# A four-direction scan network on one core: statistics loads on another queue, coefficients in pinned stages, larger scaling pieces, a prologue that loads first

## The chip, the cores and the metric

The kernel runs on one core of a Trainium2 chip. The core has TensorE (PE, matrix products), VectorE (DVE), ScalarE (ACT) and GpSimd (POOL). SyncE (SP) issues DMA copies; ACT issues some too, from its own queue, in the order of its own instructions. The metric is the device time of one execution in microseconds (us). The profile is of one execution, with the time of every instruction and copy.

## The reference

The input is x[32, 48, 64, 128] (batch, channel, row, column), float32. Two layers follow each other, each x = x + scan(gn(x)). gn is a group norm: 16 groups of 3 channels, mean and variance over channels, rows and columns of one batch entry. The scan has four sweeps; a step of a sweep adds to its input a 1-d convolution (5 taps, 48 to 48 channels) of the step before, along the other axis:

```python
def step(w, b):
    def f(carry, inp):
        nxt = inp + _conv1d(carry, w, b)
        return (nxt, nxt)
    return f
...
_, d_rest = jax.lax.scan(step(down_w, down_b), d0, xs[1:])      # down the rows
...
_, u_rest = jax.lax.scan(step(down_w, down_b), u0, seq)         # up the rows
...
_, r_rest = jax.lax.scan(step(right_w, right_b), r0, ws[1:])    # right over the columns
...
_, l_rest = jax.lax.scan(step(left_w, left_b), l0, R[Ww - 2::-1])  # left
...
x = x + _L0_conv_ref(_gn(x), ...)
x = x + _L1_conv_ref(_gn(x), ...)
```

Every step needs the one before it, so a sweep is a chain of 63 steps (rows) or 127 steps (columns).

## The kernel before

The 32 batch entries are 4 groups of 8. A pass is one layer of one group; there are 8 passes, layer 0 first. In a pass come 63 down steps, 63 up steps, 127 right and 127 left steps (`scans`, L505). A row step (`row_step`, L443) is 9 matmuls of 128x128 by 128x128 and 3 DVE operations that add the input row (L462). A column step works in two halves of 4 batch entries, each 3 matmuls (L476 to L480) and one DVE operation (L483).

One large SBUF tile, `arena`, holds the data of a pass. For rows it is read as `rows`, 64 rows of 384 numbers on 128 partitions. For columns it is read as `cols`, which begins 20 rows further (SHIFT) and has another layout on 112 partitions. So after the up sweep `hand_over` (L364) copies rows into `cols` by DMA, arena to arena, 20 copies (two parities of the row, ten pieces) for 8 rows; the last ones are split (`SPLITS`) at rows 4, 2 and 0. The parity r = 1 goes out on ACT's queue if the chunk ends at row 8 or below, all else on SP.

Around the scans stand helpers, Python generators that are advanced at given steps. `prepare` (L298) loads x of the next layer-0 group, reorders it with POOL copies (L331) from tiles `nat` to `perm` and stores it to DRAM as `xin`. `input_moments` and `result_moments` (L270, L285) load the data again into `perm` and let ACT sum values and squared deviations (`collect`, L190), with two small POOL operations (L199, L200) between. `scaling` (L212) turns these into a scale and an offset: small DVE operations, matmuls with a group mask (L223, L241) and a square root on ACT (L255). `fetch` (L347) loads a chunk of rows into the arena from `xin` (layer 0) or `mid` (layer 1) and scales it in place with 24 ACT operations (L356), one for each of 3 row blocks and 8 batch entries. `drain` (L491) adds the residual of the pass before in 16 steps during the next pass's row sweeps: it loads a piece into `nat`, adds on POOL (L382, L388) and stores to `mid` or to the output. Each drain step gives free 2048 numbers of `cols`, 5.3 rows, and the late fetches (rows 20 to 63) follow it. Rows 0 to 19 are outside `cols` and are fetched earlier, in the column sweeps. The last pass has `last_residual` (L402) in place of a drain.

Program order isn't the order of execution. A planner (the Tile framework's scheduler) simulates the program when it is built and fixes the order of each engine and queue: of the instructions that its simulation has ready it takes the one that comes first in the program. So an operation can stand far ahead of its place; in the profile the statistics loads of group 2, written in pass 1, start at 713.7 us, in pass 0's column sweeps. On the chip each engine and each queue then keeps that order and waits where something is late.

Of the kernel before, what the change touches and what calls it, by code (L numbers as in the profile page):

```python
# [30 lines left out]
F32 = mybir.dt.float32  # L31
# [11 lines left out]
GB = 8  # L43
# [9 lines left out]
LOADS = tuple(slice(a, b) for a, b in ((0, 4), (4, 12), (12, 20))) + tuple(  # L53
    slice(a, min(a + 8, 64)) for a in range(20, 64, 8)
)
EARLY = 3
SPLITS = {4: 8, 2: 4, 0: 2}
# [28 lines left out]
def kernel(  # L86
# [93 lines left out]
    class Moments:  # L180


        def __init__(self, parts: int, n: int, key: str):
            self.T, self.n, self.key = parts, n, key
            mean = stat_tile(GB * parts, f"mean{parts}", key)
            dev2 = stat_tile(GB * parts, f"dev2{parts}", key)
            self.mean = mean.rearrange("p (b t) -> p b t", t=parts)
            self.dev2 = dev2.rearrange("p (b t) -> p b t", t=parts)

    def collect(mo, t: int, views, key: str):  # L190


        bs = slice(min(views), max(views) + 1)
        for b, view in views.items():
            nc.scalar.activation(  # L195
                view, view, AF.Identity, scale=sides, accum_out=mo.mean[:, b, t : t + 1]
            )
        neg = stat_tile(GB, "neg", key)
        nc.gpsimd.tensor_scalar(neg[:, bs], mo.mean[:, bs, t], -1.0 / mo.n, None, ALU.mult)  # L199
        nc.gpsimd.tensor_scalar(  # L200
            mo.mean[:, bs, t], mo.mean[:, bs, t], 1.0 / mo.n, None, ALU.mult
        )
        for b, view in views.items():
            nc.scalar.activation(  # L204
                view,
                view,
                AF.Square,
                bias=neg[:, b : b + 1],
                accum_out=mo.dev2[:, b, t : t + 1],
            )  # L210

    def scaling(mo):  # L212

        key, T = mo.key, mo.T
        ps = ps_stat.tile([FULL, NG + 1, 2 * GB], F32, tag="ps_stat", name=f"ps_{key}")
        pair = stat_tile(2 * GB, "pair", key)
        if T > 1:
            total = stat_tile(GB, "total", key)
            nc.vector.tensor_reduce(total, mo.mean, mybir.AxisListType.X, ALU.add)
            nc.vector.tensor_scalar(pair[:, 0:GB], total, 1.0 / T, None, ALU.mult)  # L220
        else:
            nc.vector.tensor_copy(pair[:, 0:GB], mo.mean[:, :, 0])  # L222
        nc.tensor.matmul(ps[0:P, NG, 0:GB], mask_sb, pair[:, 0:GB], start=True, stop=True)  # L223
        mean_p = stat_tile(GB, "mean_p", key)
        nc.vector.tensor_copy(mean_p, ps[0:P, NG, 0:GB])
        dev = stat_tile(GB * T, f"dev{T}", key).rearrange("p (b t) -> p b t", t=T)
        nc.vector.tensor_tensor(
            dev, mo.mean, mean_p.unsqueeze(2).to_broadcast([P, GB, T]), ALU.subtract
        )
        sq = stat_tile(GB * T, f"sq{T}", key).rearrange("p (b t) -> p b t", t=T)  # L230
        nc.vector.tensor_tensor(sq, dev, dev, ALU.mult)
        all_sq = stat_tile(GB * T, f"all{T}", key).rearrange("p (b t) -> p b t", t=T)
        nc.vector.scalar_tensor_tensor(all_sq, mo.dev2, 1.0 / mo.n, sq, ALU.mult, ALU.add)
        if T > 1:
            total2 = stat_tile(GB, "total2", key)
            nc.vector.tensor_reduce(total2, all_sq, mybir.AxisListType.X, ALU.add)
            nc.vector.tensor_scalar(pair[:, GB:], total2, 1.0 / T, None, ALU.mult)
        else:
            nc.vector.tensor_copy(pair[:, GB:], all_sq[:, :, 0])
        for o in range(NG):  # L240
            nc.tensor.matmul(ps[:, o], maskp[:, o], pair, start=True, stop=True)  # L241
# [7 lines left out]
        var = small("var")  # L249
        nc.vector.tensor_scalar(var, ps[:, 0:NG, GB:], GN_EPS, None, ALU.add)  # L250
        mean = small("mean")
        nc.vector.tensor_copy(mean, ps[:, 0:NG, 0:GB])

        std = small("std")
        nc.scalar.activation(std, var, AF.Sqrt)  # L255
        r0 = small("r0")
        nc.vector.reciprocal(r0, std)
        t0 = small("t0")
        nc.vector.tensor_tensor(t0, var, r0, ALU.mult)
        t1 = small("t1")  # L260
        nc.vector.tensor_tensor(t1, t0, r0, ALU.mult)
        t2 = small("t2")
        nc.vector.tensor_scalar(t2, t1, -0.5, 1.5, ALU.mult, ALU.add)
        scale = small("scale", 2 * NGRP)
        nc.vector.tensor_tensor(scale, r0, t2, ALU.mult)
        offset = small("offset", 2 * NGRP)
        nc.vector.scalar_tensor_tensor(offset, mean, -1.0, scale, ALU.mult, ALU.mult)
        return scale, offset

    def input_moments(g: int):  # L270

        parts, n = 2, H * W // 4
        mo = Moments(parts, n, f"x{g}")
        coeffs[0, g] = mo
        for b in range(GB):
            for t in range(parts):
                tile_ = perms[t].rearrange("p r n -> p (r n)")
                flat = x[g * GB + b].rearrange("c (s t h) w -> s t c (h w)", s=2, t=parts)
                for s in range(2):
                    nc.sync.dma_start(tile_[SIDES[s]], flat[s, t])  # L280
                collect(mo, t, {b: tile_}, f"x{g}_{b}{t}")
                yield
        coeffs[0, g] = scaling(mo)

    def result_moments(g: int):  # L285

        mo = Moments(NCH, W * CH, f"m{g}")
        src = stages[1][g].rearrange("(q r) c n -> r c q n", r=2)
        for j in range(NCH):
            t = perms[j % 2]  # L290
            for r in range(2):
                nc.sync.dma_start(t[SIDES[r]], src[r, :, CH * j : CH * (j + 1)])
            view = t.rearrange("p q (n b) -> p b (q n)", b=GB)
            collect(mo, j, {b: view[:, b] for b in range(GB)}, f"m{g}_{j}")
            yield
        coeffs[1, g] = scaling(mo)

    def prepare(g: int):  # L298

        first = g == 0
        if first:
            at = H * ROW + 7 * CH * PAIR
            st = arena[0:P, at : at + GB * NCH * 6].rearrange(
                "p (b j k) -> p b j k", b=GB, j=NCH
            )
        for j in range(NCH):
            nat, perm = nats[j % 2], perms[j % 2]
            if first and j >= 2:  # L310
                at = H * ROW + CH * PAIR * (j - 2 if j < 9 else j - 16)
                nat = arena[0:P, at : at + CH * PAIR].rearrange("p (r n) -> p r n", r=CH)
                eng = nc.vector if j % 2 else nc.gpsimd
                eng.memset(nat[32:64], 0.0)
            h0 = 2 * CH * j
            nat = nat.rearrange("p r n -> p (r n)").rearrange("p (b n) -> p b n", b=GB)
            for s in range(2):
                h = h0 + s * CH
                nc.sync.dma_start(
                    nat[SIDES[s]],  # L320
                    x[g * GB : (g + 1) * GB, :, h : h + CH].rearrange(
                        "b c h w -> c b (h w)"
                    ),
                )
            if first:
                for b in range(GB):
                    nc.vector.bn_stats(st[:, b, j, :], nat[:, b])
            nat = nat.rearrange("p b (r k e) -> p r e k b", r=CH, e=E8)
            perm5 = perm.rearrange("p r (e k b) -> p r e k b", e=E8, k=NK)
            for r in range(CH):  # L330
                nc.gpsimd.tensor_copy(perm5[:, r], nat[:, r])  # L331
            for s in range(2):
                h = h0 + s * CH
                nc.sync.dma_start(
                    stages[0][g][h : h + CH].rearrange("h c n -> c h n"), perm[SIDES[s]]
                )
            yield
        if first:
            mo = Moments(1, 1, "x0")
            mv = stat_tile(2 * GB, "mv", "x0").rearrange("p (b k) -> p b k", k=2)  # L340
            for b in range(GB):
                nc.vector.bn_aggr(mv[:, b], st[:, b].rearrange("p j k -> p (j k)"))
            nc.vector.tensor_copy(mo.mean[:, :, 0], mv[:, :, 0])
            nc.vector.tensor_copy(mo.dev2[:, :, 0], mv[:, :, 1])
            coeffs[0, 0] = scaling(mo)

    def fetch(layer: int, g: int, j: int, scale, offset):  # L347

        hs = LOADS[j]
        src = stages[layer][g][hs].rearrange("h c (e n) -> e c h n", e=E8)  # L350
        for e, c0, c1, o, p0 in PIECES:
            nc.scalar.dma_start(rows[p0 : p0 + c1 - c0, hs, o], src[e][c0:c1])
        view = rows[:, hs].rearrange("p h o (k b) -> p o b h k", b=GB)
# [10 lines left out]
    def hand_over(h0: int, h1: int):  # L364

        qs = slice(h0 // 2, h1 // 2)
        for r in range(2):
            eng = nc.scalar if r and h1 <= RB else nc.sync
            src = rows[:, h0:h1].rearrange("p (q r) o n -> r o p q n", r=2)
            dst = cols[SIDES[r], qs].rearrange("p q e k b -> e p q (k b)")  # L370
            for e, c0, c1, o, p0 in PIECES:
# [161 lines left out]
    for _ in prepare(0):  # L533
        pass
# [111 lines left out]
```

## Time and profile before

| what | value |
|---|---|
| median of 3 runs | 5951.42 us (5949.96 to 5955.78) |
| the profiled execution | 5961.04 us, span 5959.3 us |
| busy: PE, DVE, ACT, POOL | 4860.6, 2548.1, 1812.3, 1087.5 us |
| mean granted TensorE clock | 0.922 |
| DMA | 599.97 MB, mean 101 GB/s |
| first row step | 229.7 us |
| last column step ends | 5810.4 us |

The stages are read from PE's instructions by tile: `row_01d` is layer 0, group 1, down; `col_12r` is layer 1, group 2, right. Sweeps in us:

| pass | down | up | gap | right | left |
|---|---|---|---|---|---|
| 00 | 138.5 | 126.8 | 55.9 | 173.5 | 170.4 |
| 01 | 146.3 | 126.8 | 45.1 | 172.1 | 170.4 |
| 02 | 146.3 | 126.8 | 44.9 | 173.1 | 170.4 |
| 03 | 155.3 | 127.7 | 47.2 | 172.7 | 240.6 |
| 10 | 148.6 | 126.8 | 46.4 | 226.4 | 170.4 |
| 11 | 170.5 | 126.8 | 50.9 | 172.0 | 232.5 |
| 12 | 169.2 | 126.8 | 52.8 | 172.7 | 170.4 |
| 13 | 171.7 | 126.8 | 48.3 | 172.7 | 170.4 |

A busy share is an average over stages with different limits; what a change in one stage is worth is read from that stage. Waits are put down to what ended last.

### The profile page before, as it was taken

How to read it: one execution, taken by the hardware profiler on the slowest of the kernel's cores; microseconds unless marked ns; L12 is line 12 of the kernel's file. 1: busy time of each engine (PE TensorE's matmuls, PEld its weight loads, DVE VectorE, ACT ScalarE, POOL GpSimd, SP SyncE). 2: the span in 40 equal slices, each digit the busy share in tenths (PEclk: the TensorE clock that was granted, in tenths of full speed). 3: DMA queues.
4: the chain of work that ended last, by engine and by line, in shares of the span. 5: the costliest groups of instructions: out<-in, count | busy, mean ns of one | idle time of the engine just before them, and what ended most of it. 6: DMA issues, size and time to landing. Idle time of an engine off the chain costs nothing. (4 is left out here: it accounts for less than half of the span.)

```text
span 5959.3 us, 105466 instructions
## 1 busy us (share of the span) xinstructions
PE 4860.6 (82%) x42592; PEld 4846.2 (81%) x42592; DVE 2548.1 (43%) x7387; ACT 1812.3 (30%) x3977; POOL 1087.5 (18%) x640
## 2 busy tenths in 40 slices
PE   0496999889996998795997969869698799986990
PEld 0496999889996998795997969869698799986990
DVE  3343554445443553342543535335354345433550
ACT  0451234024220396077050840308603020220000
POOL 3101303121221303000030001510015100350043
PEclk9998999999998999897998989989799899998995
DMA  7665838477465738442184412754117510463045
GB/s 149 118 114 108 174 64 184 106 155 151 98 158 109 167 66 192 111 84 54 22 184 109 84 19 44 149 122 83 30 34 151 121 37 1 95 129 89 1 69 92
DMA packets 847369, 599.97 MB, mean 101 GB/s; under 512 B 267584, under 2 KB 783680, under 8 KB 842272
## 3 DMA queue, kind: packets, MB, share of 16 engines
q1 hardware_dynamic: 603840, 483.73, 39.7%
q10 hardware_dynamic: 243040, 109.49, 9.5%
q8 instruction: 335, 5.49, 0.4%
q14 instruction: 154, 1.26, 0.1%
HBM read 341.31 MB, written 150.99 MB: 83 GB/s over the span
## 5 line engine op out<-in xcount | busy, mean ns | idle before, releaser
L356 ACT ACTIVATE arena<-arena,offset_m,scale_m 128x128 f32<-128x128 f32 (+1 forms) x864 | 425.6, 584 | 1243.6 <-DMA arena<-mid 895.1
L356 ACT ACTIVATE arena<-arena,offset_x,scale_x 128x128 f32<-128x128 f32 (+1 forms) x864 | 422.4, 590 | 901.2 <-DMA arena<-xin 738.6
L195 ACT ACTIVATE perm<-perm,sides 112x256 f32<-112x256 f32 (+1 forms) x560 | 476.2, 858 | 577.1 <-DMA perm<-in_x 192.4
L388 POOL TENSOR_TENSOR perm<-arena,nat 112x1024 f32<-112x1024 f32 x96 | 360.8, 3785 | 1154.8 <-DVE arena L483 459.7
L382 POOL TENSOR_TENSOR nat<-arena,nat 112x2048 f32<-112x2048 f32 x64 | 289.2, 4533 | 671.5 <-DMA nat<-xin 353.9
L204 ACT ACTIVATE perm<-perm,neg_m 112x256 f32<-112x256 f32 x512 | 381.0, 752 | 13.7 <-POOL neg_m L199 13.7
L331 POOL COPY perm<-nat 112x1024 f32<-112x1024 f32 x100 | 200.0, 2034 | 646.7 <-DMA nat<-in_x 599.8
L199 POOL TENSOR_SCALAR neg_m<-mean_m 112x8 f32<-112x8 f32 x64 | 15.1, 236 | 1250.1 <-ACT perm L195 1250.1
L424 POOL TENSOR_TENSOR perm<-arena,nat 112x256 f32<-112x256 f32 x108 | 114.4, 1067 | 485.4 <-DVE arena L483 328.1
L223 PE MATMUL ps_x<-pair_x,mask_sb 112*112 112x8 f32 x8 | 1.6, 276 | 237.2 <-DVE pair_x L222 221.4
L223 PEld LDWEIGHTS ps_x<-pair_x,mask_sb 112*112 112x112 f32 x8 | 1.5, 231 | 237.4 <-DVE pair_x L222 221.4
L476 PE MATMUL col_10r<-arena,wc 112*112 112x128 f32 x508 | 106.3, 292 | 97.3 <-DVE arena L483 50.9
L454 PE MATMUL row_13d<-arena,wd 128*128 128x128 f32 x1134 | 141.7, 291 | 30.0 <-DVE arena L462 30.0
L454 PEld LDWEIGHTS row_13d<-arena,wd 128*128 128x128 f32 x1134 | 139.1, 206 | 32.5 <-DVE arena L462 32.5
L454 PE MATMUL row_11d<-arena,wd 128*128 128x128 f32 x1134 | 137.7, 286 | 29.9 <-DVE arena L462 29.9
L454 PEld LDWEIGHTS row_11d<-arena,wd 128*128 128x128 f32 x1134 | 135.2, 201 | 32.0 <-DVE arena L462 32.0
L454 PE MATMUL row_12d<-arena,wd 128*128 128x128 f32 x1134 | 138.6, 287 | 27.7 <-DVE arena L462 27.7
L454 PEld LDWEIGHTS row_12d<-arena,wd 128*128 128x128 f32 x1134 | 136.0, 202 | 29.8 <-DVE arena L462 29.8
L476 PE MATMUL col_03l<-arena,wc 112*112 112x128 f32 x508 | 105.5, 290 | 67.2 <-DVE arena L483 67.2
L476 PE MATMUL col_11l<-arena,wc 112*112 112x128 f32 x508 | 105.4, 290 | 59.2 <-DVE arena L483 59.2
L454 PE MATMUL row_03d<-arena,wd 128*128 128x128 f32 x1134 | 137.1, 286 | 18.2 <-DVE arena L462 18.2
L454 PEld LDWEIGHTS row_03d<-arena,wd 128*128 128x128 f32 x1134 | 135.2, 201 | 20.0 <-DVE arena L462 19.8
(228 smaller groups left out, 13956.7 us busy)
## 6 DMA issues: line engine op xcount, KB each, us to landing
arena<-arena SPq DMA_DIRECT2D x672, 96.0 KB, 2.5
xin<-perm SPq DMA_DIRECT2D x128, 384.0 KB, 5.2
nat<-xin SPq DMA_DIRECT2D x128, 384.0 KB, 8.6
mid<-nat SPq DMA_DIRECT2D x128, 384.0 KB, 5.1
perm<-mid SPq DMA_DIRECT2D x128, 384.0 KB, 6.3
nat<-in_x SPq DMA_DIRECT2D x100, 384.0 KB, 8.0
perm<-in_x SPq DMA_DIRECT2D x96, 384.0 KB, 6.3
nat<-mid SPq DMA_DIRECT2D x96, 384.0 KB, 6.9
```

The costliest lines, as they stand in the source:

```text
L195: nc.scalar.activation(view, view, AF.Identity, scale=sides, accum_out=mo.mean[:, b, t : t + 1])
L199: nc.gpsimd.tensor_scalar(neg[:, bs], mo.mean[:, bs, t], -1.0 / mo.n, None, ALU.mult)
L204: nc.scalar.activation(view, view, AF.Square, bias=neg[:, b : b + 1], accum_out=mo.dev2[:, b, t : t + 1],)
L223: nc.tensor.matmul(ps[0:P, NG, 0:GB], mask_sb, pair[:, 0:GB], start=True, stop=True)
L331: nc.gpsimd.tensor_copy(perm5[:, r], nat[:, r])
L356: nc.scalar.activation(view[:, o, b], view[:, o, b], AF.Identity, bias=offset[:, o, b : b + 1], scale=scale[:, o, b : b + 1],)
L382: nc.gpsimd.tensor_tensor(nat, res, nat, ALU.add)
L388: nc.gpsimd.tensor_tensor(perm[:, t].rearrange("p (b k e) -> p b k e", b=GB, k=NK), cols[:, q + t].rearrange("p e k b -> p b k e"), nat[:, ...
L424: eng.tensor_tensor(perm[:, t].rearrange("p (b k e) -> p b k e", b=GB, k=kn), cols[:, q + t, :, ks].rearrange("p e k b -> p b k e"), nat[: ...
L454: nc.tensor.matmul(ps[o][:, a:b], wd[:, n], prev[:, i, a + s * GB : b + s * GB], start=seen[o] == 1, stop=seen[o] == left[o],)
L476: nc.tensor.matmul(ps, wt[:, 1], prev, start=True, stop=False)
```

## The change

- Statistics loads (`input_moments`, `result_moments`) are issued from ACT's queue, `fetch`'s loads from SP's. `collect` negates the mean with one ACT operation in place of two on POOL.
- `scaling` becomes a generator of eight stages. Its PE and DVE instructions are put behind the latest step's last matmul and DVE operation in the planner's order (`tc.issue_after`, which sets order and no wait). It is advanced in the right sweep from i = 60 (passes 0 to 3) or in the row sweeps from t = 30 (from pass 4 on).
- The pieces that `fetch` scales become (0, 4), (4, 12), (12, 20), (20, 28), (28, 44), (44, 64). Its loads are still of 8 rows at most. A late piece is fetched, as before, after the drain step that frees its last row; the first three are advanced at i = 100, 80, 60 of the left sweep (before: 95, 63, 31).
- `hand_over` splits the end further: rows 4 to 7, 2 to 3, 1, 0. Only the chunks of rows 1 and 0 use ACT's queue, for every second piece.
- `prepare` of group 0 becomes `prepare_first`: all loads first, then statistics, reordering and stores.
- The drain advances at t % 5 after t = 27 (before: 6), the moments at t % 6 (before: 7).

```diff
-LOADS = tuple(slice(a, b) for a, b in ((0, 4), (4, 12), (12, 20))) + tuple(
-    slice(a, min(a + 8, 64)) for a in range(20, 64, 8)
-)
+LOADS = ((0, 4), (4, 12), (12, 20), (20, 28), (28, 44), (44, 64))
 EARLY = 3
-SPLITS = {4: 8, 2: 4, 0: 2}
+SPLITS = {4: 8, 2: 4, 1: 2, 0: 1}
...
-        nc.gpsimd.tensor_scalar(neg[:, bs], mo.mean[:, bs, t], -1.0 / mo.n, None, ALU.mult)
-        nc.gpsimd.tensor_scalar(
-            mo.mean[:, bs, t], mo.mean[:, bs, t], 1.0 / mo.n, None, ALU.mult
-        )
+        nc.scalar.mul(mo.neg[:, bs, t], mo.sum[:, bs, t], -1.0 / mo.n)
...
+    @contextmanager
+    def behind_steps():
+        with ExitStack() as stack:
+            for ins in mark.values():
+                stack.enter_context(tc.issue_after(ins))
+            yield
+
+    def scaling(mo, layer: int, g: int):
         key, T = mo.key, mo.T
+        with behind_steps():
+            pair = stat_tile(2 * GB, "pair", key)
             total = stat_tile(GB, "total", key)
+            nc.vector.tensor_reduce(total, mo.sum, mybir.AxisListType.X, ALU.add)
+            nc.vector.tensor_scalar(
+                pair[:, 0:GB], total, 1.0 / (T * mo.n), None, ALU.mult
+            )
+        yield
+        with behind_steps():
+            ps = ps_stat.tile(
+                [FULL, NG + 1, 2 * GB], F32, tag="ps_stat", name=f"ps_{key}"
+            )
+            nc.tensor.matmul(
+                ps[0:P, NG, 0:GB], mask_sb, pair[:, 0:GB], start=True, stop=True
+            )
+        yield
...
+            std = small("std")
+            nc.scalar.activation(std, var, AF.Sqrt)
+        yield
+        yield
...
+        coeffs[layer, g] = scale, offset
...
-                    nc.sync.dma_start(tile_[SIDES[s]], flat[s, t])
-                collect(mo, t, {b: tile_}, f"x{g}_{b}{t}")
+                    nc.scalar.dma_start(tile_[SIDES[s]], flat[s, t])
+                collect(mo, t, {b: tile_})
...
-                nc.sync.dma_start(t[SIDES[r]], src[r, :, CH * j : CH * (j + 1)])
+                nc.scalar.dma_start(t[SIDES[r]], src[r, :, CH * j : CH * (j + 1)])
...
+    def prepare_first():
...
+        for j, nat in enumerate(tiles):
+            take_in(0, j, nat)
+        for j, nat in enumerate(tiles):
...
+            for b in range(GB):
+                nc.vector.bn_stats(st[:, b, j, :], by_batch[:, b])
+            restage(0, j, nat)
...
+        for _ in scaling(mo, 0, 0):
+            pass
+
+    def fetch(layer: int, g: int, j: int):
+        scale, offset = coeffs[layer, g]
+        h0, h1 = LOADS[j]
+        for h in range(h0, h1, RB):
+            hs = slice(h, min(h + RB, h1))
+            src = stages[layer][g][hs].rearrange("h c (e n) -> e c h n", e=E8)
+            for e, c0, c1, o, p0 in PIECES:
+                nc.sync.dma_start(rows[p0 : p0 + c1 - c0, hs, o], src[e][c0:c1])
+        view = rows[:, h0:h1].rearrange("p h o (k b) -> p o b h k", b=GB)
...
     def hand_over(h0: int, h1: int):
-        qs = slice(h0 // 2, h1 // 2)
-        for r in range(2):
-            eng = nc.scalar if r and h1 <= RB else nc.sync
...
+        for h in range(h0, min(h1, h0 + 2)):
+            q0, r = divmod(h, 2)
+            qs = slice(q0, max((h1 - r + 1) // 2, q0 + 1))
...
+            for i, (e, c0, c1, o, p0) in enumerate(PIECES):
+                eng = nc.scalar if i % 2 and h1 <= 2 else nc.sync
+                eng.dma_start(dst[e][c0:c1], src[o][p0 : p0 + c1 - c0])
...
-            while loads and (i >= first or LOADS[loads[0]].stop <= free):
-                fetch(*nxt, loads.pop(0), *coeffs[nxt])
+            while loads and (i >= first or LOADS[loads[0]][1] <= free):
+                fetch(*nxt, loads.pop(0))
...
-                if (t % 3 == 0) if t <= 27 else t % 6 == 0:
-                    advance(side, "drain")
-                if t % 7 == 1:
-                    advance(side, "moments")
+                if (t % 3 == 0) if t <= 27 else t % 5 == 0:
+                    advance("drain")
+                if t % 6 == 1:
+                    advance("moments")
+                if t == 30 and n >= NGRP:
+                    if (1, n - NGRP + 1) in moments:
+                        ready = (1, n - NGRP + 1)
+                        side["scaling"] = scaling(moments[ready], *ready)
+                if t % 2:
+                    advance("scaling")
...
+                if i == 60 and n < NGRP:
+                    side["scaling"] = scaling(moments[ready], *ready)
+                if i % 4 == 0:
+                    advance("scaling")
...
-                if nxt and i % 32 == 31 and i < 96:
-                    fetch(*nxt, 2 - i // 32, *coeffs[nxt])
+                if nxt and i in (100, 80, 60):
+                    fetch(*nxt, (100, 80, 60).index(i))
```

## The prediction

> **What bounds the kernel now.** I read the busy row first, then PE's waits, then a stage table, then the timelines of the stages that lose time. All times are of the one profiled execution: 5961.0 us by the clock around it, 5959.3 us of span. The median shown is 5951.4, so I subtract 9.6 us at the end.
>
> PE is busy 82% of the span, and its instructions by tile give a floor. An undisturbed pass is 126.8 us down, 126.8 up, 172 right and 170.4 left. What lies above that floor is: 229.7 us before the first row step, eight idle stretches between up and right (391 us in all, mean 49), 148.9 us after the last column step, some 200 us of longer down sweeps, and three long holes inside column sweeps.
>
> ```profile
> PE col_03l L476 <- DVE arena L483: 67.2, 1, 67.2
> PE col_11l L476 <- DVE arena L483: 59.2, 1, 59.2
> PE col_12r L476 <- DMA arena<-arena: 52.7, 1, 52.7
> PE col_10r L476 <- DVE arena L483: 50.9, 1, 50.9
> ...
> PE col_01r L476 <- DMA arena<-arena: 45.1, 1, 45.1
> ```
>
> In each line: who waited for whom, us in total, times, longest. Those that name L483 are holes inside column sweeps; those that name a copy within the arena are the idle stretches before right. The timeline of DVE shows what filled the first one: a reduction of the group-norm statistics was placed ahead of the column step and waited for POOL.
>
> ```profile
> 2789.51 0.29 DVE L219 TENSOR_REDUCE total_m<-mean_m 112x8 f32<-112x128 f32 x1 [67.35 <-POOL mean_m L200]
> ```
>
> The stage table (span, busy time and count of PE, PEld, DVE, ACT, POOL, then clock, DMA share, GB/s) gives the prologue, a layer-0 down sweep and a layer-1 down sweep:
>
> ```profile
> 0.00:229.70 229.70, 2.05 (x9) 1.85 (x9) 70.38 (x167) 4.84 (x11) 76.78 (x44) 1.00 0.85 165
> 894.30:1040.60 146.30, 132.28 (x1146) 131.70 (x1145) 69.58 (x203) 71.67 (x145) 54.25 (x12) 0.95 0.91 187
> 5120.90:5292.60 171.70, 141.70 (x1138) 139.19 (x1137) 61.80 (x189) 71.65 (x144) 86.75 (x24) 0.88 0.74 148
> ```
>
> The prologue and the layer-0 sweep are near full on DMA. The layer-1 sweep is not. There POOL's additions of the previous pass's residual come one pair per 15 us though a pair takes 7.5, since a load of the next one sits behind the stores on SP:
>
> ```profile
> 5182.21 7.44 POOL L388 TENSOR_TENSOR perm<-arena,nat 112x1024 f32<-112x1024 f32 x2 [7.14 <-issue]
> 5199.07 7.63 POOL L388 TENSOR_TENSOR perm<-arena,nat 112x1024 f32<-112x1024 f32 x2 [9.42 <-DMA nat<-mid]
> ```
>
> Each pair frees 5.3 rows of the arena, so it paces the loads of rows 20 to 63 and their scaling. The row steps wait for that scaling: there is no slack here to give away.
>
> ```profile
> DVE arena L462 <- ACT arena L356: 113.0, 34, 6.1
> ```
>
> That is 34 waits of DVE on ACT. One such piece of 8 rows, 24 activations, in ACT's timeline:
>
> ```profile
> 5194.81 12.38 ACT L356 ACTIVATE arena<-arena,offset_m,scale_m 128x128 f32<-128x128 f32 x24 [13.15 <-DMA arena<-mid]
> ```
>
> **The change part by part.**
>
> **Prologue (229.7 us).** Today each of the 32 loads of group 0 queues on SP behind stores that wait for POOL, and statistics end at 218. With all loads ahead, 12.6 MB at the 178 to 199 GB/s of the windows from 60 us on take some 68 us, plus the weights' share of the start: 85 us. But the stores follow, and two perm buffers allow one pair of stores per 4.1 us of POOL copy (2 x 2.0, L331) plus 4.7 of landing, over two: 5 us with issue, 14 x 5 = 70. Then 10 loads of rows 0 to 3 (10 us, now SP too) and half of the 9.6 us of their scaling. That is 85 + 70 + 10 + 5 = 170. Ends: 120, if the planner slips the fetch between the stores, and 185. I take 165: -65 us (-45 to -110).
>
> **Coefficients pinned behind steps.** The three holes go: 67.2 + 59.2 + 50.9 = -177. In their place, each of seven sets puts about 14 small DVE operations of 0.2 us and 8 stages between steps; together 3 us. A small operation can also last long beside POOL:
>
> ```profile
> 974.25 2.76 DVE L227 TENSOR_TENSOR dev_x<-mean_x,mean_p_x 112x16 f32<-112x16 f32 x1
> ...
> 977.68 4.25 DVE L237 TENSOR_SCALAR pair_x<-total_x 112x8 f32<-112x8 f32 x1
> ```
>
> That set stopped PE for 9.6 us (973.8 to 983.4). Four sets now run in right sweeps, where POOL copies take 2.0: I take 5 us each, +20 (ends 12 and 38). Three run in layer-1 down sweeps from row 30, where row 44's data will be late anyway (below); they cost nothing there, 9.6 each without that cover. Sum -157 (-137 to -177).
> Here a rule speaks against the change: the Trainium skill, "SBUF — State Buffer", section "Who interferes with whom", says that a tensor_scalar, a copy or a two-input operation on SBUF loses the port for the whole GpSimd instruction. The two rows agree. Read strictly, each of the 8 stages beside POOL at half load could lose up to 4 us, about 16 us a set by that page as an estimate; then this part is 45 us worse over the four exposed sets.
>
> **Statistics loads on ScalarE's queue, and -mean on ACT.** 32 issues a pass leave SP and join ACT; ACT issues take 0.3 to 1.2 us, so 20 us a pass on an engine 30% busy. POOL loses 224 operations of 0.2 us. Both lie beside the column sweeps (342 us a pass): zero. Without that cover it is 7 x 20 us. Behind a waiting statistics load stand the next group's scalings; rows 0 to 19 have the whole right and left sweep for them, which also makes the new times 100, 80 and 60 and the drain's t % 5 free. The folded branches and reused tiles of the coefficient code keep its count of operations: zero.
>
> **Fetches on SP, larger pieces.** The 60 late loads of a pass leave ACT's queue for SP, past the drain's loads and stores. Rows 28 to 43 become one piece, rows 44 to 63 another. A piece is scaled only when its last row is in, and row 43 needs the drain's step 4, row 63 step 8. Today rows 28 to 35 start at step 2, rows 44 to 51 at step 5.
> One activation issues every 0.40 us at 64 elements and 0.51 at 128. The far row (112x256, 0.75 us against 0.61 at 128) bounds 256 elements by 0.65; extending the slope from 64 to 128 gives 0.75. So 24 of them at 256 take 16 to 18 us, at 320 some 20 us.
> Layer 0: step 8's addition ends 107 us into the sweep (894 to 1001). DMA is full, so SP order changes its pace little. Rows 60 to 63: 8 us of issue, 8 of landing, 20 of scaling, then 20 rows x 2.01 + 5 = 45 us. 107 + 36 + 45 = 188, against 146.3, 146.3, 155.3, 148.6: +156 over four sweeps (ends: 175, loads in while POOL works, +104; 205, one more round of ten issues on the drain's cycle, +224).
> Layer 1: step 8 ends at 131 (5121 to 5252). Without delay on SP: 131 + 6 + 5 + 20 + 41 = 203. With rows 20 to 43 (30 issues, each ten 7 to 10 us on ACT's queue today) ahead of the drain's next loads and 30 more issues behind step 8: 131 + 22 + 22 + 5 + 20 + 41 = 241, up to 252. If the planner instead gets the drain's loads out early, POOL's 7.5 is the pace and the sweep is 170. I take 228, near the two serial values since SP's order today is the serial one: +172 against 170.5, 169.2, 171.7 (ends 0 and +245).
> The rule in the Trainium skill, "ScalarE: Activation LUTs", section "What ACT_TABLE_LOAD costs", gives 0.833 ns an element beyond a fixed part. This trace has 1.8 ns between 64 and 128 elements of these strided rows. By the page the 320-element piece would be about 5 us shorter, 35 us over seven sweeps, as an estimate.
>
> **Hand-over.** Per pass 170 copies go out on SP and 30 on ACT; now 190 and 10. SP issues one per 0.65 us, so an SP that keeps up would start the first column step 29 us after up (50 copies after row 8, less the 16 us of rows 8 to 0, plus landing). It does not keep up today:
>
> ```profile
> 1132.42 39.94 SPq L372 DMA_DIRECT2D arena<-arena  x19
> ```
>
> 19 issues should take 12 us; 24 us of it is one wait, until a copy that ACT issued for rows 2 and 3 landed (both queues name the same nine completion semaphores in turn). Passes 0 to 4 lose 20 to 25 us so; passes 5 to 7 start 35 us late behind the drain. In the change ACT issues only for rows 0 and 1, so such a wait ends later, at the end of up, with some 85 copies left: 85 x 0.65 = 55. If it does not hit, 31. I take 52 against 49: +24 over eight (-144 to +64).
>
> **The tail** (148.9 us) is untouched: zero.
>
> Sum: -65 - 157 + 156 + 172 + 24 = +130. 5961 + 130 = 6091; less 9.6, 6081.
>
> **Rivals.**
> Hand-over freed (faster): SP keeps up without the wait on ACT's copies; -144 instead of +24 gives -38, so 5913. It decides once the gap falls below 35 us. For it: moments and the drain's end leave SP earlier. Against: the 24 us hole appears in five passes.
> Layer-1 drain prefetched (faster): sweeps of 170; 130 - 172 = -42, so 5909. For it: POOL idles 7 of 15 us. Against: 60 more issues stand on the queue that sets the pace. With the one before: about 5740.
> SP saturated (slower): the drain's cycle stretches in both layers, 205 and 252, and the gap grows to 57: 130 + 68 + 73 + 40 = +311, 6262.
> Pinning does little: the staged operations meet POOL or late statistics and half of the 177 stays: +90, 6170.
>
> **How the numbers follow.** The forecast has 0.46 (own range 6010 to 6160), hand-over 0.12, drain 0.11, both 0.05, saturated 0.15, pinning 0.07, and 0.04 that gains and losses cancel within 0.2%, about what a measurement here can tell from no change. Faster 0.28, same 0.04, slower 0.68. The range 5850 to 6270 leaves out the joint gain and the far end of saturation.
>
> **What would show it.** The first row step near 165 us; no hole above 10 us in a column sweep, and no DVE reduction waiting on another engine; layer-0 down sweeps near 188 and layer-1 near 228, with DVE's wait on ACT's scaling grown from 113 to over 300 us in two waits a sweep, at rows 28 and 44; gaps of 50 us before right. Wrong it would be by down sweeps below 160 (then SP's order is not what I think) or by gaps near 30.

## The result and the profile after

The changed kernel takes 6184.9 us (median of 4 runs, 6172.1 to 6187.3), the kernel before 5953.6 us beside it (5950.0 to 5956.8). The ratio is 1.038 with a 95% interval of 1.037 to 1.040: slower by 231 us. The profiled execution has a span of 6181.9 us, 222.6 more than before, and a mean granted clock of 0.904 in place of 0.922.

The stages, read from PE's instructions by tile as before, in us (in the second table, step 1 is the time to the first row step):

| pass | down | up | gap | right | left |
|---|---|---|---|---|---|
| 00 | 163.5 | 126.8 | 30.3 | 176.9 | 170.2 |
| 01 | 191.1 | 126.8 | 51.6 | 180.0 | 170.2 |
| 02 | 192.3 | 126.8 | 51.7 | 179.9 | 170.2 |
| 03 | 218.2 | 126.8 | 51.5 | 173.5 | 170.1 |
| 10 | 225.5 | 126.8 | 50.7 | 173.1 | 170.2 |
| 11 | 229.9 | 126.8 | 61.1 | 173.1 | 170.2 |
| 12 | 227.7 | 126.8 | 51.4 | 172.4 | 170.2 |
| 13 | 223.2 | 126.8 | 51.7 | 172.3 | 170.3 |

| sum of | step 1 | down | gap | right | left | tail | span |
|---|---|---|---|---|---|---|---|
| before | 229.7 | 1245.1 | 391.5 | 1434.0 | 1494.8 | 148.8 | 5959.3 |
| after | 183.7 | 1671.4 | 400.1 | 1401.3 | 1361.5 | 149.4 | 6181.9 |

So the holes in the column sweeps are gone (right and left -166) and the prologue is shorter (-46), while the down sweeps grew by 426. The waits of PE (who waited for whom, us in total, times, longest) say the same: no column step waits for a DVE operation for long, the copies within the arena still stand in front of each right sweep, and the row steps of the down sweeps stand at the head of the list.

```profile
PE row_13d L495 <- DVE arena L503: 88.6, 6, 35.9
PE row_11d L495 <- DVE arena L503: 85.4, 8, 33.2
PE row_03d L495 <- DVE arena L503: 83.6, 6, 32.7
...
PE col_11r L517 <- DMA arena<-arena: 61.1, 1, 61.1
...
PE col_01r L517 <- DMA arena<-arena: 51.6, 1, 51.6
...
PE col_02r L517 <- DVE arena L524: 3.5, 2, 3.1
```

Behind DVE's addition of the input row (L503, L462 before) stands ACT's scaling. Its waits were 113.0 us in 34 waits, the longest 6.1; now the number of waits has hardly grown, but the longest is eight times as long:

```profile
DVE arena L503 <- ACT arena L396: 501.3, 41, 48.9
```

They come in two groups in each down sweep from pass 01 on, as predicted: in pass 01 up to row step 28, 76 us into the sweep, and up to row step 44, at 137 us.

The stretches that answer to the three of before: the prologue, the layer-0 down sweep of pass 01, the layer-1 down sweep of pass 13 (span, busy time and count of PE, PEld, DVE, ACT, POOL, then clock, DMA share, GB/s).

```profile
0.00:183.70 183.70, 2.00 (x8) 1.80 (x8) 78.17 (x170) 6.85 (x13) 76.23 (x44) 1.00 0.78 154
851.50:1042.70 191.20, 134.52 (x1138) 132.96 (x1137) 61.16 (x189) 57.30 (x80) 58.80 (x13) 0.84 0.76 155
5288.20:5511.50 223.30, 134.69 (x1138) 133.13 (x1137) 61.27 (x189) 50.73 (x72) 97.08 (x26) 0.79 0.65 124
```

No engine has much more to do than before: PE's busy time goes from 132.3 to 134.5 us in the first sweep and from 141.7 to 134.7 in the second, POOL's grows by 5 and 10 us, ACT's falls by 14 and 21. The DMA share fell from 0.91 to 0.76 and from 0.74 to 0.65. Nothing is full: the sweeps wait in turn for one thing after another. The order is plain at the end of pass 01's drain. This is SP's timeline (start, us, instruction, count):

```profile
954.56 5.26 SPq L426 DMA_DIRECT2D mid<-nat  x4
959.86 21.37 SPq L392 DMA_DIRECT2D arena<-xin  x27
```

And this is ACT's:

```profile
981.70 20.61 ACT L396 ACTIVATE arena<-arena,offset_x,scale_x 128x320 f32<-128x320 f32 x24 [42.75 <-DMA arena<-xin]
```

The drain's eighth step is stored up to 959.8, 108 us into the sweep. Then SP issues 27 loads in 21 us, then ACT scales rows 44 to 63 in 20.6 us, and then the last 20 rows take 40 us to the sweep's end at 1042.7. POOL's pairs of additions in layer 1 still come 15 us apart, for the load of the next pair still stands behind stores on SP:

```profile
5395.60 7.49 POOL L429 TENSOR_TENSOR perm<-arena,nat 112x1024 f32<-112x1024 f32 x2 [7.23 <-DMA nat<-mid]
5410.03 7.51 POOL L429 TENSOR_TENSOR perm<-arena,nat 112x1024 f32<-112x1024 f32 x2 [6.93 <-DMA nat<-mid]
```

The reduction that stood for 67 us in a column sweep now finds its data, between two column steps:

```profile
2771.72 0.35 DVE L524 SCALAR_TENSOR_TENSOR arena<-col_03r,bc,arena 112x128 f32<-112x128 f32 x1 [0.29 <-PE col_03r L521]
2771.99 0.27 DVE L224 TENSOR_REDUCE total_m<-sum_m 112x8 f32<-112x128 f32 x1
```

The hand-over's wait on SP is there too. This is SP's timeline about the end of pass 01's up sweep (1169.4), the place of the line shown of before; at 0.70 us each, the pace of a queue that does not wait, 28 copies would take 20 us:

```profile
1138.67 43.89 SPq L413 DMA_DIRECT2D arena<-arena  x28
```

### The profile page after: what moved, and what is told of

It is laid out like the page before. It is cut to its first block, busy times and chain, and to the rows that moved or that the text cites. A ratio compares the mean times of both kernels' runs of the same rounds, so it can differ in the third digit from the quotient of the medians.

```text
span 6181.9 us, 104510 instructions
## 1 busy us (share of the span) xinstructions
PE 4866.9 (79%) x42592; PEld 4848.9 (78%) x42592; DVE 2549.4 (41%) x7390; ACT 1669.3 (27%) x3513; POOL 1034.3 (17%) x416
## 5 line engine op out<-in xcount | busy, mean ns | idle before, releaser
L396 ACT ACTIVATE arena<-arena,offset_m,scale_m 128x128 f32<-128x128 f32 (+3 forms) x576 | 340.4, 684 | 1534.8 <-DMA arena<-mid 1132.0
L396 ACT ACTIVATE arena<-arena,offset_x,scale_x 128x128 f32<-128x128 f32 (+3 forms) x576 | 341.6, 685 | 402.8 <-DMA arena<-xin 309.4
L495 PE MATMUL row_00d<-arena,wd 128*128 128x128 f32 x1134 | 140.8, 290 | 92.1 <-ACT arena L396 72.3
L495 PEld LDWEIGHTS row_00d<-arena,wd 128*128 128x128 f32 x1134 | 138.6, 205 | 94.2 <-ACT arena L396 73.0
L495 PE MATMUL row_10d<-arena,wd 128*128 128x128 f32 x1134 | 136.6, 285 | 88.6 <-DMA nat<-xin 47.7
L495 PEld LDWEIGHTS row_10d<-arena,wd 128*128 128x128 f32 x1134 | 134.5, 200 | 90.4 <-DVE arena L503 90.4
L495 PE MATMUL row_13d<-arena,wd 128*128 128x128 f32 x1134 | 134.7, 283 | 88.6 <-DVE arena L503 88.6
L495 PE MATMUL row_03d<-arena,wd 128*128 128x128 f32 x1134 | 134.7, 283 | 83.6 <-DVE arena L503 83.6
L495 PE MATMUL row_02d<-arena,wd 128*128 128x128 f32 x1134 | 135.3, 283 | 57.2 <-DVE arena L503 57.2
```

The lines of the kernel that those rows point to most:

```text
L396: nc.scalar.activation(view[:, o, b], view[:, o, b], AF.Identity, bias=offset[:, o, b : b + 1], scale=scale[:, o, b : b + 1],)
L495: mark["pe"] = nc.tensor.matmul(ps[o][:, a:b], wd[:, n], prev[:, i, a + s * GB : b + s * GB], start=seen[o] == 1, stop=seen[o] == left[o], ...
```

## The experiments

The questions were these. Which half of the fetch change lengthens the down sweeps: the larger pieces, or the loads' place on SP? What sets the gap before right? What removed the holes? And did the statistics loads on ACT cost nothing, as I had said? All versions start from the changed kernel. Ratios are to the kernel before.

### Larger pieces or the loads' queue

Three versions: pieces of 8 rows with the loads on SP; large pieces with the loads on ACT; both undone.

```diff
-LOADS = ((0, 4), (4, 12), (12, 20), (20, 28), (28, 44), (44, 64))
+LOADS = ((0, 4), (4, 12), (12, 20)) + tuple((a, min(a + 8, 64)) for a in range(20, 64, 8))
```

```diff
-                nc.sync.dma_start(rows[p0 : p0 + c1 - c0, hs, o], src[e][c0:c1])
+                nc.scalar.dma_start(rows[p0 : p0 + c1 - c0, hs, o], src[e][c0:c1])
```

> The change, with the scaling pieces of 8 rows as before; fetches stay on SP. The changed kernel's eight down sweeps last 1673 us in all, before's 1246. If the piece size is the cause (row 28 waits for row 43's data, row 44 for row 63's), they fall by 250 us or more and the time is 5900 to 5950 us, with layer-0 sweeps at 150 to 165 and layer-1 sweeps at 170 to 200. If SP's queue is the cause (30 issues on the drain's path), they fall by less than 100 us and the time stays above 6080.

> The change, with fetch's loads on ACT's queue as before; the large pieces stay. If the piece size is the cause, the down sweeps fall by at most 120 us (the drain's step 8 in layer 1 comes 25 us earlier, and only 10 issues are left behind it) and the time is 6060 or above. If SP's queue is the cause, they fall by 250 us or more and the time is at or below 5930. In either case the first row step comes earlier than 183.7 us if it waits for SP's stores: 130 to 150.

> The change, with both the 8-row pieces and fetch's loads on ACT's queue. Both theories: the down sweeps go back to 1250 to 1290 us and the time to 5760 to 5800, as only the gains of the pinned coefficients and of the prologue are left. If it is above 5880, something else in the change lengthens the down sweeps (the statistics loads on ACT's queue beside passes 3 and 4 are the candidate).

| version | us | ratio, 95% | step 1 | down | gap |
|---|---|---|---|---|---|
| after | 6184.9 | 1.038 (1.037 to 1.040) | 183.7 | 1671.4 | 400.1 |
| small pieces | 6014.7 | 1.010 (1.008 to 1.012) | 181.9 | 1355.2 | 547.4 |
| loads on ACT | 5906.1 | 0.991 (0.989 to 0.993) | 125.6 | 1477.6 | 370.7 |
| both | 5806.0 | 0.974 (0.973 to 0.976) | 129.9 | 1249.6 | 494.3 |

Neither theory alone holds. Small pieces take 316 us off the down sweeps, loads on ACT 194, both together 422: that is back to within 5 us of the 1245.1 of before, so without these two edits the growth does not come, and they overlap by 88. (Some of it needs the statistics loads on ACT too, as the third part shows.) The version with both undone is 6 us above what I had expected. The loads' queue also costs 58 us in the prologue, where the fetch of rows 0 to 3 stands behind group 0's stores on SP:

```profile
109.01 59.30 SPq L341 DMA_DIRECT2D xin<-perm  x26
168.36 15.65 SPq L392 DMA_DIRECT2D arena<-xin  x11
```

What I had not expected is the gap column; for small pieces I had named 5900 to 5950 us. With small pieces the down sweep of pass 01 ends 48 us earlier, but the drain's last steps do not: they now run 50 us into the up sweep, and only then does SP begin its copies. This is SP's timeline in pass 01 with small pieces (up from 982.4 to 1109.2, first column step at 1163.9):

```profile
1032.07 132.90 SPq L413 DMA_DIRECT2D arena<-arena  x190
```

190 copies at 0.70 us are longer than the up sweep (126.8), so the first column step comes when SP is through. Of the 316 us saved 147 come back as gaps.

### The gap before right

Every hand-over copy on SP, first in the changed kernel, then with small pieces and ACT loads as well; and, with these, every second copy on ACT.

```diff
-                eng = nc.scalar if i % 2 and h1 <= 2 else nc.sync
+                eng = nc.sync
```

```diff
-                eng = nc.scalar if i % 2 and h1 <= 2 else nc.sync
+                eng = nc.scalar if i % 2 else nc.sync
```

> The change, with every hand-over copy on SP (200 a pass in place of 190 and 10 on ACT). If the gap before right (51 to 61 us in passes 1 to 7) comes from SP's wait for a copy that ACT issues at the end of up, it goes, and though SP has 10 more copies at 0.65 us the gap falls to 34 to 40 us in passes 1 to 7: time about 6080 to 6100. If SP is simply late, the gap grows by 6.5 us to 58 and the time is about 6230.

> 8-row pieces and fetch's loads on ACT (5806 us), and every hand-over copy on SP. Gaps before right are 52 to 57 in layer 0 and 62 to 86 in layer 1 there. If the wait for ACT's last copies sets them in layer 0 and the drain's end (40 to 50 us into up) in layer 1, layer 0's fall to 33 to 37 and layer 1's stay or grow by up to 7: 5730 to 5770 us. If one cause sets both, layer 1's fall by 15 to 20 too: below 5690.

> 8-row pieces, fetch's loads on ACT, and every second hand-over copy of every chunk on ACT's queue (100 copies on each queue a pass). If the issue time of 0.65 us on one queue sets the gap, both queues keep up with the rows (10 copies, 6.5 us, per 16 us): gaps of 10 to 20 us in all passes, time 5410 to 5520. If the shared semaphores tie the two queues together whatever their load, gaps stay above 40 and the time above 5700.

| version | us | ratio, 95% | down | gap | gaps of 01 to 03 | gaps of 11 to 13 |
|---|---|---|---|---|---|---|
| all on SP | 6103.0 | 1.025 (1.023 to 1.027) | 1672.0 | 322.5 | 32 to 33 | 40 to 64 |
| small, ACT loads, all on SP | 5776.8 | 0.971 (0.970 to 0.973) | 1258.6 | 469.0 | 38 to 57 | 65 to 87 |
| small, ACT loads, both queues | 5528.0 | 0.929 (0.928 to 0.931) | 1256.5 | 201.5 | 14 to 21 | 21 to 24 |

The first row is the wait by itself: ten copies in 200 moved from ACT to SP, and the down sweeps are unchanged while the gaps fall by 78 and the right sweeps by 12. In the same stretch SP now issues 49 copies in 36 us, without a stop:

```profile
1139.24 35.74 SPq L413 DMA_DIRECT2D arena<-arena  x49
```

The trace also has what ties the two queues together. The record of a DMA issue names the semaphore that its landing will count up, and the semaphores that it waits for first. There are eight of the first kind, which SP's and ACT's issues share. In pass 01 of the changed kernel SP stands from 1148 us until 1172.00, before an issue that counts on semaphore 100 and waits for it first; ACT's copy on semaphore 100, issued at 1170.16, landed at 1171.98.

The gap that is left in layer 0, 31 to 33 us, is what I had named for an SP that keeps up; in layer 1 it is 40 to 64. The second row shows that the wait is not all: once the sweeps are short, SP's own pace and its late start set the gap, above all in layer 1. Less came of it than I expected: passes 01 and 02 fall to 38, but pass 03 stays at 57, and why was not looked into. The third row tests that: with the copies dealt to two queues from the start, the gaps fall to 14 to 24 in seven of eight passes. Only pass 00's gap did not fall (62.3, with a right sweep of 202.8), where ACT also had the next group's statistics loads. My figure for this version, at most 5520, was 8 us too low.

The Trainium skill, "Trainium Kernel Development and Optimization", section "Key Constraints", says that issuing DMAs from several engines only saves the sequencer's issue time, since all share 16 DMA engines. Here that saving was the gap: dealing the same copies to two queues took 267 us off the gaps (469.0 to 201.5).

### What removed the holes, and what the statistics loads cost

The pins taken out (the staged operations stay where they are written); the statistics loads put back on SP; both.

```diff
-            for ins in mark.values():
-                stack.enter_context(tc.issue_after(ins))
             yield
```

```diff
-                    nc.scalar.dma_start(tile_[SIDES[s]], flat[s, t])
+                    nc.sync.dma_start(tile_[SIDES[s]], flat[s, t])
...
-                nc.scalar.dma_start(t[SIDES[r]], src[r, :, CH * j : CH * (j + 1)])
+                nc.sync.dma_start(t[SIDES[r]], src[r, :, CH * j : CH * (j + 1)])
```

> The change without its pins: scaling stays in eight stages at the same places of the program, but nothing is queued behind the steps. If the pins removed the holes of 50 to 67 us in the column sweeps, they come back, at least three of them: 6340 to 6380 us. If the place in the program is enough, no column sweep is longer than 181 us and the time stays at 6185, within 20.

> The change with the statistics loads back on SP's queue. In passes 03 and 10 the down sweeps are 218 and 226 us against 191 in 01 and 02, and ACT works on statistics during them. If the loads on ACT's queue cause this (SP waits for a completion semaphore that such a load, late behind ACT's own work, holds), both fall to 190 to 200 and the time to 6110 to 6150. If it is ACT's work that delays the scaling, or the drain itself, they stay within 10 us and the time is 6180 or above, with SP more loaded.

> The change with the statistics loads on SP as before, and without pins. Without pins but with the loads on ACT no hole came back. If that was because the loads on ACT end the statistics earlier, the holes in column sweeps come back now, at least two of 50 us or more: 6190 to 6280 us. If the later place of scaling in the program is enough, no column sweep is longer than 181 us and the time is 6030 to 6110 (6103 with pins).

| version | us | ratio, 95% | down | gap | right | left |
|---|---|---|---|---|---|---|
| after: loads on ACT, pins | 6184.9 | 1.038 (1.037 to 1.040) | 1671.4 | 400.1 | 1401.3 | 1361.5 |
| loads on ACT, no pins | 6136.1 | 1.032 (1.030 to 1.033) | 1627.8 | 410.8 | 1380.1 | 1361.6 |
| loads on SP, pins | 6103.4 | 1.026 (1.024 to 1.028) | 1584.9 | 413.9 | 1399.9 | 1361.6 |
| loads on SP, no pins | 6274.8 | 1.053 (1.052 to 1.055) | 1563.3 | 428.2 | 1506.2 | 1431.0 |

My expectation that the holes return without pins was wrong: they did not, and the kernel was 49 us faster. With the loads on SP they do return, three of them, as in the kernel before; PE's waits of that version:

```profile
PE col_03l L515 <- DVE arena L522: 66.6, 1, 66.6
PE col_11r L515 <- DVE arena L522: 64.7, 1, 64.7
...
PE col_10r L515 <- DVE arena L522: 56.5, 1, 56.5
```

DVE's waits there name the same reduction as before, now behind ACT's sums, since the division that POOL made is gone:

```profile
DVE total_m L222 <- ACT perm L195: 188.2, 3, 66.7
```

So each of the two edits, the pins and the loads on ACT, removes the holes by itself, and the change has both. The pins are worth 171 us beside loads on SP and cost 49 beside loads on ACT. Without them the right sweeps are 21 us shorter and the down sweep of pass 10 37 us (225.5 to 188.1), and those of passes 11 to 13 together 13 us.

The loads on ACT, which I had costed at zero, cost 81 us (6184.9 to 6103.4). The down sweeps get 86 us back, of these 25.0 in pass 00, 26.7 in 03 and 27.2 in 10; the gaps lose 14: 22 in pass 00 (30.3 to 51.9), where SP now meets the wait that it had missed, less 9 won in pass 11. Two mechanisms come into question. First, with the loads on ACT statistics work stands in the down sweeps. Busy times of the down sweep of pass 03 in the changed kernel (the same columns as above):

```profile
2292.10:2510.40 218.30, 134.69 (x1138) 133.13 (x1137) 61.17 (x189) 130.25 (x287) 59.04 (x13) 0.80 0.83 161
```

and with the loads on SP:

```profile
2278.10:2469.50 191.40, 134.40 (x1136) 132.84 (x1135) 61.22 (x189) 50.79 (x72) 58.73 (x13) 0.84 0.77 151
```

ACT is busy for 130 us in place of 51. But this work does not hold up the scaling that the row steps wait for. The scaling of rows 44 to 63 takes as long in both, and ACT sits idle before it until the rows are loaded; here it is with the loads on ACT, then with the loads on SP:

```profile
2449.33 20.64 ACT L396 ACTIVATE arena<-arena,offset_x,scale_x 128x320 f32<-128x320 f32 x24 [23.51 <-DMA arena<-xin]
```

```profile
2409.16 20.62 ACT L396 ACTIVATE arena<-arena,offset_x,scale_x 128x320 f32<-128x320 f32 x24 [45.04 <-DMA arena<-xin]
```

It starts 157 us into the sweep in place of 131, and these 26 us are the sweep's 26.7. So the loss comes in front of the loads, on SP. That is the second mechanism: SP is held. Its waits in this sweep of the changed kernel have three lines for the landing of `perm<-mid`, the statistics loads that ACT issues:

```profile
SPq L426 <- DMA perm<-mid: 25.9, 3, 14.6
SPq L392 <- DMA perm<-mid: 18.1, 6, 6.4
SPq L420 <- DMA perm<-mid: 7.3, 1, 7.3
```

These are 51 us. Pass 00 has 53 us of such waits (there for `perm<-in_x`) and pass 10 has 63, and the five other down sweeps have none: the three that have them are the three that get 25 us and more shorter with the loads on SP. With the loads on SP no store and no fetch has one in these sweeps. Without the pins, pass 03 keeps them (73 us, a sweep of 223.3) and pass 10 has none and is the short one of above, 188.1. The longest single wait is in pass 10. Four stores to `mid`, 100 us into the sweep in both; in the changed kernel SP's timeline has

```profile
3132.68 22.55 SPq L426 DMA_DIRECT2D mid<-nat  x4
```

and with the loads on SP

```profile
3092.51 5.30 SPq L426 DMA_DIRECT2D mid<-nat  x4
```

The fourth store goes out only at 3154.93. It counts on semaphore 107 and waits for it first, and the DMA before it on that semaphore is a statistics load that ACT issued between two of its sums and that landed at 3154.91. ACT's timeline:

```profile
3150.05 0.31 ACTq L314 DMA_DIRECT2D perm<-mid  x1
```

So it is the shared completion semaphore of the hand-over again. How much of the delay the extra DMA traffic of these sweeps adds (a share of 0.83 against 0.77 in pass 03) was not separated.

### The parts that help, together

Small pieces, fetch on ACT, hand-over on both queues, statistics loads on SP; once with the pins and once without.

> 8-row pieces, fetch's loads on ACT, hand-over copies on both queues in turn (5528 us), and the statistics loads back on SP. If the loads on ACT cost pass 00 its long down sweep, gap and right sweep (158, 62 and 203 us there), these go to about 138, 20 and 178 and the time to 5420 to 5470. If SP pays as much for 32 more issues a pass, in gaps of more than 25 us, it stays at 5500 or above.

> The kernel with hand-over copies on both queues and statistics loads on SP, without pins. If pins only hold ACT's square roots and the statistics behind them back, it is 20 to 50 us faster than with pins. If pins keep coefficients from being waited for inside column sweeps, it is 50 us or more slower.

| version | us | ratio, 95% | step 1 | down | gap | right | left |
|---|---|---|---|---|---|---|---|
| with pins | 5494.4 | 0.923 (0.921 to 0.925) | 119.9 | 1275.8 | 174.0 | 1395.3 | 1361.5 |
| without | 5590.6 | 0.939 (0.937 to 0.941) | 128.2 | 1260.8 | 166.2 | 1411.7 | 1470.2 |

The version with pins is the fastest, 7.7% below the kernel before. It is 34 us better than with the statistics loads on ACT, less than the 81 of the changed kernel and 24 us over the top of what I expected. Pass 00 gains 49 us in its gap (39.0) and right sweep (176.8), but its down sweep, which I had expected at 138, is 163.0 (157.9 before). Pass 03 loses 25 (down 144.4 to 169.0). There SP begins with statistics loads that wait for ACT's sums:

```profile
2070.20 24.86 SPq L314 DMA_DIRECT2D perm<-mid  x5
```

The drain's first store stands behind them and goes out 34 us into the sweep in place of 5. The pins are worth 96 us here. PE's longest waits in it behind the prologue:

```profile
PE col_00r L517 <- DMA arena<-arena: 39.0, 1, 39.0
PE row_13d L495 <- DVE arena L503: 29.4, 10, 4.4
```

No row step of a later pass waits more than 9 us at once. PE is busy for 4863 us as in every version, now 89% of the span.

## Why the prediction came out as it did

The side was right and the time is in the range, 104 us above the forecast and 25 above the end of the likeliest case's own range. By its terms, made against the profiled execution (sum +130, measured +222.6, the stages rounded):

| term | predicted | measured |
|---|---|---|
| prologue | -65 | -46.0 |
| coefficients: right and left sweeps | -157 | -166.0 |
| statistics loads: pass 00's down sweep | 0 | +25.0 |
| layer-0 down sweeps 01, 02, 03, 10 | +156 | +230.6 |
| layer-1 down sweeps 11, 12, 13 | +172 | +169.4 |
| hand-over gaps | +24 | +8.6 |

**The step that failed** is "Statistics loads on ScalarE's queue", the largest term that the sum had at nothing, which I took as "beside the column sweeps: zero" with a price of 140 if that cover was gone. It was partly gone. Moving the loads back is worth 81 us, and 79 us are won in three down sweeps: pass 00, which I had at no change, and passes 03 and 10, which I had at 188 and which came to 218.2 and 225.5. I had counted ACT's share of time and what stood behind a waiting load on ACT; I had not asked in which sweep the planner would put the statistics, nor who on SP waits for a copy that ACT issues late, though I used that very wait for the hand-over. The waits of 51 to 63 us on SP in just these three sweeps are what stood in its place.

**Layer-0 sweeps** where no statistics stood are right to 4 us and by the right steps: 191.1 and 192.3 against 188. The drain's step 8 was put at 107 us and ended about 108, scaling at 20 and took 20.6. Two terms were off and cancelled: the loads' issue and landing took 22 us in place of 16, the last 20 rows 40 in place of 45. The slope that I extended from 64 to 128 elements held: the three sizes of pieces in pass 13 are

```profile
5310.55 12.34 ACT L396 ACTIVATE arena<-arena,offset_m,scale_m 128x128 f32<-128x128 f32 x24 [326.34 <-DMA arena<-mid]
5370.35 17.81 ACT L396 ACTIVATE arena<-arena,offset_m,scale_m 128x256 f32<-128x256 f32 x24 [47.47 <-DMA arena<-mid]
5451.18 20.57 ACT L396 ACTIVATE arena<-arena,offset_m,scale_m 128x320 f32<-128x320 f32 x24 [63.01 <-DMA arena<-mid]
```

which is 1.8 ns an element between any two. The Trainium skill's 0.833 ("ScalarE: Activation LUTs", "What ACT_TABLE_LOAD costs") would have made the largest some 5 us shorter, as an estimate; the measurement decides. **Layer-1 sweeps** came to 229.9, 227.7 and 223.2 against 228. That SP's order is the serial one was the choice between far ends, and it was the right one. In pass 13 the last addition of step 8 ended 144 us into the sweep, 13 later than before; the loads behind it took 19 us, scaling 20.6 and the rest 40. The runs put the cause in both edits: neither the pieces nor the queue alone gives the whole growth.

**Coefficients.** The holes went and the price was as taken: the right sweeps of passes 00 to 03 grew by 18.9 us together, against 20. In the layer-1 down sweeps, where I had them at nothing, they were not free: without them pass 10 is 37 us shorter, through the statistics that they hold back into it (ACT runs 346 instructions in that sweep with the pins, 73 without). In pass 01 three of some sixteen small operations met POOL's copies and took 0.9 to 1.9 us in place of 0.2. The strict reading of the skill's rule ("SBUF — State Buffer", "Who interferes with whom"), 16 us a set, is not what came: 3.4, 7.9, 6.8 and 0.8 us. It was stricter than the page, which gives the ports to whichever instruction issues first, and has a `tensor_scalar` or a copy contend only in the modes that use both ports. But the reason that I gave was only half of it: the pins were not needed beside the loads on ACT, and cost more than they gave there.

**Hand-over.** The wait hit as I argued: gaps of 51 to 52, and 31 to 33 without it in layer 0. (The records name eight shared semaphores, not nine.) The figure for an SP that keeps up is less sure than it looks: the 50 copies of the working give 19 us, and only with the 20 copies of rows 8 to 15, due at the same time, does it come to the 29 named. Pass 00, at 30.3, was the one that the wait missed. The baseline already had it, so the term is small. The rival in which it is freed did not come with this change. One line brings about half of it: 82 us, with gaps 69 below those of before where I had priced 144, as layer 1's stay at 40 to 64.

**Prologue.** The forecast of 165 was below the working's own 170, and the loads took longer: the last landed at 99.4 us, where I had put 85. From then on the working held: the stores, paced by POOL's copies, took some 69 us against 70, the fetch and the start of its scaling 15 against 15. The end of the range at 120 was not reached, as the planner did not slip the fetch between the stores; with the fetch on ACT's queue the first row step came at 125.6.

Of the rivals, neither the freed hand-over nor the prefetched drain came. A saturated SP (gaps of 57, sweeps of 205 and 252) came in neither layer as I described it, although two layer-0 sweeps passed 205, with SP held and not full.

## What to carry to other kernels

An engine that issues DMAs in its own instruction order is part of every queue that shares a completion wait with it: before loads are moved to an engine that is only 30% busy, ask what it will be doing when the load comes due, and who on the other queue waits for it. Where a consumer takes data row by row just behind a producer, a larger piece delays its first row by all the work of its last; the saved instructions were worth nothing next to that. And a wait that is shortened in one stage shows its worth only in the next one: here half of what shorter down sweeps saved came back as gaps, until the copies behind them were dealt to two queues.

## What was not expected of the hardware

SP issues one arena copy per 0.70 us, so the 200 of a hand-over are longer than the up sweep that should cover them. SP and ACT side by side issue at 0.77 and 0.76 us each, almost twice the rate. These are the two queues in pass 01 of the fastest version, in 26 us about the end of the up sweep (1064.5); SP's timeline

```profile
1054.71 26.36 SPq L413 DMA_DIRECT2D arena<-arena  x34
```

and ACT's

```profile
1054.41 25.10 ACTq L413 DMA_DIRECT2D arena<-arena  x33
```

The granted clock is lower in the down sweeps with more waits: 0.95 to 0.84 in the layer-0 sweep and 0.88 to 0.79 in the layer-1 sweep, against 1.00 in the up sweep of pass 01, where PE is busy throughout. PE's busy time in the layer-0 sweep rose by only 2.2 us (132.3 to 134.5) with it, and fell in the layer-1 sweep, so the lower clock is not what made the sweeps longer.
